# A mixture-of-experts layer with one Strassen level: a fourth of the first layer's block products taken by seven products of its own blocks, and squares of four slot tiles turned in one instruction

## The chip, the cores and the metric

The kernel runs on one core of one Trainium2 chip, in float32. The metric is the device time in microseconds (us) of one execution. Before the change it is 1579.84 us, the median of 3 runs (1579.2 to 1580.43).

## The reference

What is computed, cut to what matters: every token's vector of 512 is rotated as a set of quaternions (a 4 x 4 linear map of its four quarters of 128), a gate picks 2 of 8 experts for it, each expert takes up to 1024 tokens through two layers, and the weighted results are added to the input.

```python
# x: (4, 1024, 512); N = 4096 tokens, E = 8 experts, K = 2, D = 512, H = 2048
x_filtered = ifft(fft(x_quat, axis=1) * spectral_gate, axis=1).real    # gate is constant in time
x_rotated  = hamilton(q_left_n, hamilton(x_filtered, q_right_conj))    # 4 x 4 map per quarter
logits = xf @ gate_w.T
topv, topi = top_k(softmax(logits), K);  gates = topv / sum(topv)
cap = int(K * ((N + E - 1) // E))                                      # 1024 slots per expert
loc, valid = place of each choice in its expert's slots, loc < cap
de = slots filled with the rotated tokens                              # (E, cap, D)
h  = relu(einsum('ecd,ehd->ech', de, fc1_w) + fc1_b)                   # (E, cap, H)
eo = einsum('ech,ehd->ecd', h, fc2_w) + fc2_b                          # (E, cap, D)
out = x + sum over k of gates * valid * eo[slot of choice k]
```

## The kernel before

**Groups and products.** Each expert's hidden dimension of 2048 is cut into 4 groups of 512 (g = 0 to 3), so there are 32 groups, numbered k = 0 to 31, k = 4 e + g. In each group both layers are one level of Strassen's scheme: a matrix is cut into 2 x 2 blocks, and seven block products, numbered 0 to 6, take the place of eight. Group 0 alone takes its first layer in plain products (`layer1_plain`, L967). A scheme needs four sums of blocks on each side: `left1` (L133 to L143, GpSimd) makes them of the first layer's weights, the tiles `s`; `Slots.factors` makes those of the expert's rotated tokens with `sums` (L120, GpSimd) once per expert; `right2` (L190, also by `sums`, L126 to L129, tiles `t`) makes those of the second layer's weights. The sums on the hidden side, s1 to s4, are made by `chain` (L816 to L822, VectorE, lines L818 to L821) out of the first layer's blocks h11, h21, h22 and r12 (1024 columns each in two halves m = 0, 1).

**The first layer of a group**, `layer1` (L887), is a generator of 14 units. Units 0 and 1 take product 0 (`half`, L894 to L903, its matmuls at L896: 128 x 128 weights against 512 columns) and ScalarE writes it with its bias to h11 (L911). Products 5 and 6 go on into the same two PSUM banks a[0] and a[1] in units 2, 3 and 4, 5, each written out by ScalarE, to r12 and h21. Units 6 and 7 take product 4 into banks b, which VectorE adds to r12 (L918) and to h22 (L919). Products 1, 3 and 2 are not whole block products: each is again taken by seven products of the blocks of its own blocks, with 256 columns each. The class `Within` (L829) does this in four steps on one PSUM bank: `one` (2 products), `two` and `third`, `three`, `four` (2 products), all matmuls at L839, and after each its adds by VectorE at L850, seven in all. The bank's half a is used by `one`, then `two`, `three` and `four` accumulate on, so a step waits for the adds of the step ahead of it. A further bank c holds `third` of two such products side by side, in halves of one tile. The sums that these inner products need are made by `left_sub` (L147, GpSimd, tiles `sub13` and `sub2`, lines L162 to L165) and, once per expert, by `right_sub` (L172, VectorE, tiles `xsub`, L182 to L185). Products 1 and 3 run as a pair in units 8 to 11, product 2 follows in units 10 to 13.

**The second layer**, `second_layers` (L1125), is a second generator. It takes a group in two halves, st0 = 0 and 2, of seven units each: product 1 (with the add at L1165), 5 (L1169), 4, 6 (L1191, L1193), then product 0 of the next half (`start`, L1131, add at L1137), 3 (L1217) and 2 (L1220). All its matmuls are at L805, 256 columns each, and one unit is four of them. Product 0 of group k starts at unit 0 of the first layer of group k + 1: the second layer is one group behind.

**The order.** No scheduler orders the instructions; the program order is the order of the engines' queues. The main loop (L1246 to L1254) takes one unit of the first layer, then one of the second, and so on. After each of these half units it calls `turn(n)`, which pops n items of the list `background` and always one of the list `fetches`. `background` holds VectorE work: the four sums of `chain`, put at its head; the weighing and the store of finished rows (`Rows.store`: L681 on VectorE, then a scatter, L686, an indirect DMA issued by GpSimd); and the steps that rotate the next expert's tokens (`Slots.steps`): for half = 0, 1 of the slots and each quarter j of four, `squares(j)` turns four tiles of 128 x 128, one for each slot tile, into the one bank of the pool ps_x (L736), and then for i = 0 to 3 the bank, weighted by a number of the map, is written (j = 0: ScalarE, L774) or added (VectorE, L776) to part i of the rotated tokens. `fetches` holds indirect gathers issued by GpSimd: the next expert's rows in quarters (L721), the choices (L662) and the rows of the output (L632), to which the weighed results are added before they go back. How many items of `background` go where is a table, `PACE` (L1235 to L1239), of three rows (the first for k % 4 = 0 and for k = 1, the second for other k with k % 4 = 1, the third for k % 4 = 2 and 3), by unit, and by which of the two generators has just run. (In groups 0 and 31 one is popped each time.)

**What stands where around the change.** With g the group of the first layer: the steps of half 0 are appended to `background` at unit 11 of g = 1, those of half 1 at unit 9 of g = 2 (L1102). The finished rows of an expert, whose last group the second layer ends in the next expert's g = 0 and g = 1, are popped as stores by the same list. The quarters are appended to `fetches` at unit 12 of g = 0 and of g = 1 (L1100), the choices where the second layer begins its group 1 (L1151). `left_sub` of group k is called ahead of that group's units, one step after each of units 0 to 7 (L1086), with the steps of `right_sub` two by two in units 2 to 7 where g = 0 or k = 1 (L1088); the steps of `left1` for the group after are called in units 10 to 13, in g = 3 each with one of `Slots.factors` (L1105). Of `right2` for the next group, the first three sums are called just ahead of product 0 of that group (L1199) and the fourth after product 2 (L1222).

**Buffers.** SBUF: the rows gathered for a slot tile lie in 8 rotating tiles of 128 x 512 (`xgp`, L615, L630), `hidden` in 11 tiles of two banks' width (`unused`, L644: a block's tile is handed back by its last reader), w1 and w2 in two each, all sums on the left in one each. PSUM: the pool ps_1 has 4 banks (a, b, and those of `Within`), ps_2 3 banks (second layer), ps_x one bank.

Of the kernel before, what the change touches and what calls it, by code (L numbers as in the profile page):

```python
# [38 lines left out]
P = 128  # L40
D = 512
# [25 lines left out]
def kernel(  # L67
# [79 lines left out]
    def left_sub(k, w, s4):  # L147

        G = nc.gpsimd
        both = wsum.tile([P, 2, 4, P], F32, tag="sub13", name=f"sub13_{k}")  # L150
        one = wsum.tile([P, 1, 4, P], F32, tag="sub2", name=f"sub2_{k}")
        factors, steps = {}, []
        for t, block, names in ((both, w[:, :, 1], (1, 3)), (one, s4.unsqueeze(1), (2,))):

            def b(m, c, block=block):
                return block[:, :, c, m * P : (m + 1) * P]

            def q(i, t=t):
                return t[:, :, i]

            steps += [
                lambda b=b, q=q: G.tensor_tensor(q(0), b(1, 0), b(1, 1), ALU.add),  # L162
                lambda b=b, q=q: G.tensor_tensor(q(1), q(0), b(0, 0), ALU.subtract),
                lambda b=b, q=q: G.tensor_tensor(q(2), b(0, 0), b(1, 0), ALU.subtract),
                lambda b=b, q=q: G.tensor_tensor(q(3), b(0, 1), q(1), ALU.subtract),  # L165
            ]
            for n, name in enumerate(names):
                order = (b(0, 0), b(0, 1), q(3), b(1, 1), q(0), q(1), q(2))
                factors[name] = [f[:, n] for f in order]
        return factors, steps  # L170

    def right_sub(pool, e, right):  # L172

        factors, steps = {}, []
        for n in (1, 3, 2):
            t = pool.tile([P, 4, HS], F32, tag=f"xsub{n}", name=f"xsub{n}_{e}")

            def b(c, h, block=right[n]):
                return block[:, c, h * HS : (h + 1) * HS]

            steps += [
                lambda b=b, t=t: V.tensor_tensor(t[:, 0], b(0, 1), b(0, 0), ALU.subtract),  # L182
                lambda b=b, t=t: V.tensor_tensor(t[:, 1], b(1, 1), t[:, 0], ALU.subtract),
                lambda b=b, t=t: V.tensor_tensor(t[:, 2], b(1, 1), b(0, 1), ALU.subtract),
                lambda b=b, t=t: V.tensor_tensor(t[:, 3], b(1, 0), t[:, 1], ALU.subtract),  # L185
            ]
            factors[n] = [b(0, 0), b(1, 0), b(1, 1), t[:, 3], t[:, 0], t[:, 1], t[:, 2]]
        return factors, steps
# [426 lines left out]
    xgp = ctx.enter_context(tc.tile_pool(name="xgp", bufs=8))  # L615
# [13 lines left out]
    def gather(e, st, src):  # L629
        t = xgp.tile([P, D], F32, tag="rows", name=f"rows_{e}_{st}")  # L630
        s = e * SLOTS + st
        nc.gpsimd.indirect_dma_start(  # L632
            out=t,
            out_offset=None,
            in_=src,
            in_offset=bass.IndirectOffsetOnAxis(ap=slot_tok[:, s : s + 1], axis=0),
        )
        return t
# [12 lines left out]
    class Rows:  # L651
# [17 lines left out]
        def gather_rows(self, st):  # L669
            assert self.e == E - 1 or STORED.index(st) in turned_of[self.e + 1]  # L670
            self.rows[st] = gather(self.e, st, out)
# [27 lines left out]
    class Slots:  # L699


        def __init__(self, e):
# [5 lines left out]
            self.xg = {}  # L708
            self.rotated = 0

        def gather(self, half):
            self.xg[half] = [gather(self.e, st, x) for st in range(half * PER, (half + 1) * PER)]

        def gather_quarters(self, half, st, q):

            if q == 0:
                assert self.e == 1 or STORED[half * PER + st] in stored[self.e - 2]
                t = xgp.tile([P, D], F32, tag="rows", name=f"xq_{self.e}_{half}_{st}")
                self.xg.setdefault(half, []).append(t)
            s = self.e * SLOTS + half * PER + st  # L720
            nc.gpsimd.indirect_dma_start(  # L721
                out=self.xg[half][st][:, q * P : (q + 1) * P],
# [12 lines left out]
        def turn_squares(self, half, j, st, t):  # L735
            V.transpose(  # L736
                t[:, st * P : (st + 1) * P].rearrange("p (q w) -> p q w", w=CW),
# [564 lines left out]
```

## Time and profile before

One profiled execution of the program, taken by the hardware profiler:

| | |
|---|---|
| median of 3 runs (range) | 1579.84 us (1579.2 to 1580.43) |
| the profiled execution's own time | 1579.49 us |
| its span, first to last instruction | 1577.7 us |
| mean granted clock of TensorE in it | 0.987 |
| matmul pieces at L805 (second layer, 256 columns) | 3584 (1536, 1016, 512, 504 and 16 at the end) |
| of these the group a<-t,hidden | 364.1 us busy, 380 ns each |
| matmul pieces at L896 (512 columns), a<-x,s | x496, 592 ns each |
| weight loads, all groups shown | 190 or 191 ns each |
| L138 to L141, the sums of `left1` (GpSimd, 128 x 512) | 31 of each, 1.27 to 1.28 us |
| L126 to L129, the sums of `right2` (GpSimd, 128 x 512) | 32 of each, 1.52 to 2.06 us |
| L162, `left_sub` on two blocks (GpSimd, 128 x 256) | x31, 1.24 us |
| L721, quarters (GpSimd, indirect DMA) | x224, 1.03 us of issue each, 2.5 us from issue to landing |
| L818 to L821, `chain` (VectorE, 128 x 1024) | 32 of each, 1.55 to 1.86 us |
| L1165, L1193, L1220 and others of the second layer (VectorE) | 0.69 us each |

How to read it: the busy time of an engine counts its data instructions, the share is of the span. Matmuls overlap in TensorE's pipeline, so that one's duration (380 ns for 256 columns) is longer than the distance to the next. Every matmul of the program in float32 shows as two pieces in the trace, each with a weight load (PEld) of its own. "x" ahead of a number counts pieces or instructions. "<-PE w L839" behind an idle time names what the engine waited for: the tile w written by TensorE at line 839; "<-issue" is time in which it waited for nothing that the profile shows. Tile names are cut to the program's name without its number: w is the bank of a `Within`, c that of a pair, a and b the banks of whole products, `hidden` any block of the hidden layer, `sub` and `xsub` the inner sums, s and t the outer ones.

From 82.3 us, where the preparation (gate, choice and places of the tokens) is over, to about 1540 us TensorE runs through the 31 groups with no break that the trace shows beyond about 0.25 us at one place in each expert; an expert takes 188.2 us, a group 47.05 us.

### The profile page before, as it was taken

To read this page: it belongs to the slowest core of one execution; us is meant where nothing else is said; L and a number is where in the kernel's file an instruction comes from. 1 tells how busy PE (TensorE), PEld (TensorE's weight loads), DVE (VectorE), ACT (ScalarE), POOL (GpSimd) and SP (SyncE) were. 2 spreads that over 40 slices of the span, in tenths; PEclk is the share of its full clock that TensorE was granted. 3 is DMA by queue.
4 is the path that set the end of the run, shared out by engine and by line. 5 is a ranking of instruction groups with operands and counts; after the bars stand their busy time and mean duration, and the time that the engine had idled before them with its cause. 6 is when DMAs were issued, how large, how long until landed. Compare 5 with 4: busy or idle time off the path is not lost.

```text
span 1577.7 us, 17039 instructions
## 1 busy us (share of the span) xinstructions
PE 1544.9 (98%) x6221; PEld 1155.3 (73%) x6221; DVE 1175.9 (75%) x2082; ACT 283.7 (18%) x390; POOL 1076.5 (68%) x993
## 2 busy tenths in 40 slices
PE   5899999999999999999999999999999999999997
PEld 3667777777777777777777777777777777777776
DVE  6569877698776887688776887768867688776655
ACT  3222211112112111122111221111211121111110
POOL 1677676886768856788468866688576886665415
PEclk7899999999999999999999999999999999999999
DMA  8442112321221213220133210332122221321003
GB/s 322 160 173 77 54 45 91 117 76 54 100 94 63 73 54 114 103 99 14 53 122 121 83 56 10 124 113 81 54 82 78 92 72 54 114 106 39 16 27 105
DMA packets 48012, 137.46 MB, mean 87 GB/s; under 512 B 9335, under 2 KB 9591, under 8 KB 42809
## 3 DMA queue, kind: packets, MB, share of 16 engines
q1 hardware_dynamic: 22800, 75.54, 13.0%
q0 software_dynamic: 20736, 52.32, 10.5%
q10 hardware_dynamic: 4392, 8.52, 1.4%
q8 instruction: 49, 0.80, 0.2%
q14 instruction: 35, 0.28, 0.1%
HBM read 119.77 MB, written 25.23 MB: 92 GB/s over the span
## 4 chain that ended last, share of the span: by engine, by line
PE 95%; DMA 2%; issue 1%; POOL 1%; DVE 1%; SPq 0%; POOLq 0%; DVEq 0%
PE a L805 27%; PE b L805 20%; PE a L896 20%; PE w L839 13%; PE b L896 7%; PE c L839 5%; PE p L986 2%; DMA xb<-in_xt_dram 1%; DMA rows<-out_dram,slot_tok 0%; POOL rows L632 0%; POOL out_dram L686 0%; DMA rows<-in_x_dram,slot_tok 0%; SPq L229 0%; DVE A L504 0%; PE tok_ps L515 0%
## 5 line engine op out<-in xcount | busy, mean ns | idle before, releaser
L805 PE MATMUL a<-t,hidden 128*128 128x256 f32 x1536 | 364.1, 380 | 0.8 <-DVE v L1191 0.8
L805 PEld LDWEIGHTS a<-t,hidden 128*128 128x128 f32 x1536 | 292.7, 191 | 80.6 <-issue 40.7
L721 POOL DMA_INDIRECT xq<-in_xq_dram,quarter x224 | 231.0, 1031 | 56.1 <-issue 45.8
L805 PE MATMUL b<-w,hidden 128*128 128x256 f32 x1016 | 240.5, 380 | 2.4 <-DVE acc L1217 2.4
L805 PEld LDWEIGHTS b<-w,hidden 128*128 128x128 f32 x1016 | 193.2, 190 | 55.1 <-issue 27.7
L896 PE MATMUL a<-x,s 128*128 128x512 f32 x496 | 233.1, 592 | 0.0
L911 ACT ACTIVATE hidden<-a,b_sb 128x512 f32<-128x512 f32 x186 | 127.9, 688 | 575.2 <-PE a L896 575.2
L850 DVE TENSOR_TENSOR hidden<-w,hidden 128x256 f32<-128x256 f32 x465 | 191.0, 419 | 46.6 <-PE w L839 42.4
L827 ACT ACTIVATE hidden<-hidden 128x1024 f32<-128x1024 f32 x93 | 98.4, 1058 | 605.7 <-DVE hidden L850 357.6
L896 PEld LDWEIGHTS a<-x,s 128*128 128x128 f32 x496 | 94.2, 190 | 66.1 <-issue 59.8
L686 POOL DMA_INDIRECT out_dram<-rows,slot_add x64 | 66.6, 1041 | 109.9 <-DVE rows L681 99.1
L805 PEld LDWEIGHTS a<-w,hidden 128*128 128x128 f32 x512 | 97.3, 190 | 39.7 <-issue 29.7
L805 PE MATMUL a<-w,hidden 128*128 128x256 f32 x512 | 121.0, 379 | 0.0
L805 PE MATMUL b<-t,hidden 128*128 128x256 f32 x504 | 119.1, 379 | 0.0
L141 POOL TENSOR_TENSOR s<-w,s 128x512 f32<-128x512 f32 x31 | 39.5, 1276 | 115.3 <-PE w L839 115.1
L896 PE MATMUL b<-x,s 128*128 128x512 f32 x248 | 116.5, 592 | 0.0
L896 PE MATMUL a<-xa,w 128*128 128x512 f32 x248 | 116.4, 592 | 0.0
L805 PEld LDWEIGHTS b<-t,hidden 128*128 128x128 f32 x504 | 95.8, 190 | 26.2 <-issue 14.6
L138 POOL TENSOR_TENSOR s<-w 128x512 f32<-128x512 f32 x31 | 39.6, 1278 | 98.3 <-PE b L896 98.1
L839 PE MATMUL w<-xsub,sub 128*128 128x256 f32 x372 | 105.6, 379 | 0.0
L918 DVE TENSOR_TENSOR hidden<-b,hidden 128x512 f32<-128x512 f32 x62 | 42.5, 685 | 72.7 <-PE b L896 72.7
L850 DVE TENSOR_TENSOR hidden<-c,hidden 128x256 f32<-128x256 f32 x186 | 78.6, 423 | 21.3 <-PE c L839 15.8
(213 smaller groups left out, 2412.6 us busy)
## 6 DMA issues: line engine op xcount, KB each, us to landing
w<-in_w_dram SPq DMA_DIRECT2D x64, 1024.0 KB, 7.4
xb<-in_xt_dram SPq DMA_DIRECT2D x8, 1024.0 KB, 12.2
out_dram<-in_x_dram ACTq DMA_DIRECT2D x1, 8192.0 KB
xq<-in_xq_dram,quarter POOLq DMA_INDIRECT x224, 2.5
b<-in_b_dram POOLq DMA_DIRECT2D x8, 256.0 KB, 3.6
c<-choice,slot_cho POOLq DMA_INDIRECT x64, 2.3
rows<-out_dram,slot_tok POOLq DMA_INDIRECT x64, 3.6
out_dram<-rows,slot_add POOLq DMA_INDIRECT x64, 2.8
```

The lines of the kernel that those rows point to most:

```text
L138: lambda: G.tensor_tensor(s[0], w[:, 1, 0], w[:, 1, 1], ALU.add),
L141: lambda: G.tensor_tensor(s[3], w[:, 0, 1], s[1], ALU.subtract),
L686: nc.gpsimd.indirect_dma_start(out=out_of[st], out_offset=bass.IndirectOffsetOnAxis(ap=slot_add[:, s : s + 1], axis=0), in_=self.rows[st], ...
L721: nc.gpsimd.indirect_dma_start(out=self.xg[half][st][:, q * P : (q + 1) * P], out_offset=None, in_=xq, in_offset=bass.IndirectOffsetOnAxis ...
L805: nc.tensor.matmul(out[m] if isinstance(out, list) else out[:, m], lhsT=factors[0][n][:, c, (st0 + m) * P : (st0 + m + 1) * P], rhs=factor ...
L827: nc.scalar.activation(h, h, AF.Relu)
L839: nc.tensor.matmul(out, lhsT=self.left[n], rhs=self.right[n], start=first, stop=True, skip_group_check=True,)
L850: V.tensor_tensor(to, out, to, ALU.add)
L896: nc.tensor.matmul(out, lhsT=factors[0][n][:, c, m * P : (m + 1) * P], rhs=factors[1][n][:, c, :], start=first and c == 0, stop=c == 1, sk ...
L911: nc.scalar.activation(to[:, m], a[m], AF.Identity, bias=bias[:, m : m + 1])
L918: V.tensor_tensor(r12[:, m], b, r12[:, m], ALU.add)
L986: nc.tensor.matmul(ps[n][m][:, at], lhsT=w[:, block, i // 2, i % 2, m * P : (m + 1) * P], rhs=x.of(half, i)[:, at], start=i == 0 and at.st ...
```

## The change

**Products.** Product 6 of the first layer, so far a whole block product, becomes the fourth that is taken by seven products of its own blocks. It now forms a pair with product 1, in units 4 to 7 (`pair((1, h11), (6, h21))`); product 4 moves from units 6 and 7 to units 8 and 9; a second pair of products 3 and 2 takes units 10 to 13. After product 5 the bank a[m] is read twice by ScalarE, into r12 with one bias and into h21 with the other.

```diff
-        taken = []
-        for n, bias in ((0, lo), (5, lo), (6, hi)):
-            to = unused.pop(0)
-            taken.append(to)
-            for m in range(2):
-                half(a[m], m, n, n == 0)
-                nc.scalar.activation(to[:, m], a[m], AF.Identity, bias=bias[:, m : m + 1])
-                yield
-        h11, r12, h21 = taken
+        h11 = unused.pop(0)
+        for m in range(2):
+            half(a[m], m, 0, True)
+            nc.scalar.activation(h11[:, m], a[m], AF.Identity, bias=lo[:, m : m + 1])
+            yield
+        r12, h21 = unused.pop(0), unused.pop(0)
+        for m in range(2):
+            half(a[m], m, 5, False)
+            nc.scalar.activation(r12[:, m], a[m], AF.Identity, bias=lo[:, m : m + 1])
+            nc.scalar.activation(h21[:, m], a[m], AF.Identity, bias=hi[:, m : m + 1])
+            yield
+
+        def pair(*of):
+
+            p, q = (Within(h, subs[0][n], subs[1][n], f"w{n}_{k}") for n, h in of)
+            p.one()
+            q.one()
+            p.one_added()
+            q.one_added()
+            yield
+            c = bank1(f"c{of[0][0]}_{k}")
+            p.two()
+            p.third(c[:, :HS], True)
+            q.two()
+            q.third(c[:, HS:], False)
+            p.two_added()
+            q.two_added()
+            yield
+            p.three()
+            q.three()
+            p.three_added()
+            q.three_added()
+            yield
+            p.four()
+            q.four()
+            p.four_added()
+            q.four_added()
+
+        yield from pair((1, h11), (6, h21))
+        relu(h11)
+        yield
         h22 = unused.pop(0)
...
+        yield from pair((3, h21), (2, r12))
         relu(h21)
```

**Inner sums.** `left_sub` now makes the four sums of one block at a time (128 x 128, GpSimd), for the products 1, 6, 3 and 2 (tiles `sub1`, `sub6`, `sub3`, `sub2`); `right_sub` likewise on VectorE, with product 6 added. Those for 1 and 6 are called a group ahead, in units 9 to 13 of the group before; those for 3 and 2 in units 2 to 9. The sums of `left1` come in units 8, 9, 10 and 13, in the order 3rd, 1st, 2nd, 4th.

```diff
+        lefts, right_subs = {}, {}
+        TURN_OF_SUM = {8: 2, 9: 0, 10: 1, 13: 3}
...
+                for n, block, turns in ((3, w1_of[k][:, 1, 1], (2, 3, 4, 5)), (2, left_f[2], (6, 7, 8, 9))):
+                    lefts[n], more = left_sub(k, n, block)
+                    later(more, turns)
                 if k == 1 or g == 0:
-                    right_subs, more = right_sub(xtp, e, xf)
...
+                    for n, turns in ((6, (2, 2, 3, 3)), (3, (4, 4, 5, 5)), (2, (6, 7, 8, 9))):
+                        right_subs[n], more = right_sub(xtp, e, n, xf[n])
+                        later(more, turns)
...
+                    if i == 8 and k + 1 < NK:
+                        lefts[1], more = left_sub(k + 1, 1, w1_of[k + 1][:, 0, 1])
+                        later(more, (9, 10, 11, 12))
+                        lefts[6], more = left_sub(k + 1, 6, left_n[6])
+                        later(more, (10, 11, 12, 13))
+                        if g == NG - 1:
+                            right_subs[1], more = right_sub(xtp, e + 1, 1, xf_n[1])
+                            later(more, (8, 9, 9, 12))
...
-                if i in (10, 11, 12, 13):
-                    assert per == 1 or nxt.rotated == 2 * NJ
-                    for f in steps[:per]:
-                        f()
-                    steps = steps[per:]
+                if k and left_n and i in TURN_OF_SUM:
+                    steps[TURN_OF_SUM[i]]()
+                if k and fill_n and i >= 10:
+                    assert nxt.rotated == 2 * NJ
+                    fill_n.pop(0)()
```

Here `later(steps, turns)` puts each step behind the unit given for it.

**Squares.** The 8 rotating tiles of rows become two tiles of four slot tiles each, and the four turns of a quarter become one instruction of 128 x 512:

```diff
-    xgp = ctx.enter_context(tc.tile_pool(name="xgp", bufs=8))
+    xgp = ctx.enter_context(tc.tile_pool(name="xgp", bufs=1))
...
+    slots_of = [xgp.tile([P, PER, D], F32, name=f"rows{half}") for half in range(2)]
...
-        def turn_squares(self, half, j, st, t):
+        def turn_squares(self, half, j, t):
             V.transpose(
-                t[:, st * P : (st + 1) * P].rearrange("p (q w) -> p q w", w=CW),
-                self.xg[half][st].rearrange("p (q j w) -> p j q w", q=QT, j=NJ)[:, j],
+                t.rearrange("p (a w) -> p a w", w=CW),
+                slots_of[half].rearrange("p s (q j w) -> p j (s q) w", q=QT, j=NJ)[:, j],
             )
...
-                for st in range(PER):
-                    self.turn_squares(half, j, st, bank[j])
+                self.turn_squares(half, j, bank[j])
```

**Order.** In `chain`, r12's tile is handed back after s3 instead of s4. The choices' gathers are appended at g = 2 instead of g = 1, `right2`'s first three sums are called after product 3 (L1217) instead of ahead of product 0 of the next group, and the table is new:

```diff
-            if g == 1 and st0 == 0:
+            if g == 2 and st0 == 0:
                 r = rows[e] = Rows(e)
...
-    LATE = [(0, 0), (0, 1), (0, 0), (0, 1), (0, 1), (0, 1)]
     PACE = (
-        [(1, 1)] * 2 + [(1, 0)] * 4 + [(0, 0)] * 3 + [(0, 1), (0, 0), (0, 0), (0, 1), (0, 1)],
-        [(1, 1)] * 6 + [(0, 1), (1, 0)] + LATE,
-        [(1, 1)] * 2 + [(2, 2)] * 4 + [(0, 1), (1, 0)] + LATE,
+        [(1, 1), (1, 0)] + [(0, 1)] * 2 + [(0, 0), (0, 1)] + [(0, 0)] * 5 + [(0, 1), (0, 1), (0, 1)],
+        [(1, 1)] * 4 + [(0, 1), (1, 1), (0, 0)] + [(0, 1)] * 4 + [(1, 1)] + [(0, 1)] * 2,
+        [(1, 1), (1, 1), (2, 2), (2, 2), (0, 1), (2, 2), (0, 0), (0, 1), (1, 1), (1, 1), (0, 1)]
+        + [(1, 1), (0, 1), (0, 1)],
     )
```

In the program this makes the following of the counts: matmuls 3166 to 3259, VectorE's tensor_tensor 1421 to 1670, its transposes 226 to 58, GpSimd's tensor_tensor 535 to 783; ScalarE's instructions and the DMAs stay the same in number.

## The prediction

> **What bounds the kernel now.** I read the page from the top: busy shares, the clock row, the chain that ended last.
>
> ```profile
> span 1577.7 us, 17039 instructions
> PE 1544.9 (98%) x6221; PEld 1155.3 (73%) x6221; DVE 1175.9 (75%) x2082; ACT 283.7 (18%) x390; POOL 1076.5 (68%) x993
> PEclk7899999999999999999999999999999999999999
> PE 95%; DMA 2%; issue 1%; POOL 1%; DVE 1%; SPq 0%; POOLq 0%; DVEq 0%
> ```
>
> PE is on the chain for 95% of the span and its clock is full except at both ends. Since matmul ends are modelled, I next take starts, from the timeline of PE in a middle group:
>
> ```profile
> 699.10 1.89 PE L805 MATMUL b<-w,hidden 128*128 128x256 f32 x8
> 700.83 1.88 PE L896 MATMUL a<-x,s 128*128 128x512 f32 x4
> 702.55 1.89 PE L805 MATMUL b<-w,hidden 128*128 128x256 f32 x8
> 704.27 1.88 PE L896 MATMUL a<-x,s 128*128 128x512 f32 x4
> ```
>
> Start to start, eight 256-wide pieces take 1.72-1.73 us (215 ns each) and four 512-wide ones 1.72 us (430 ns each); one matmul of the program is two pieces. There is no gap, so PE streams and price goes by columns. What the other engines have left is read by stretches, one per group of an expert (g = 3, 0, 1, 2):
>
> ```profile
> 549.10:596.10 47.00, 47.00 (x188) 35.34 (x187) 38.47 (x67) 8.46 (x11) 25.36 (x20) 1.00 0.12 45
> 596.10:643.20 47.10, 47.10 (x188) 35.47 (x187) 35.31 (x60) 7.30 (x9) 32.55 (x30) 1.00 0.32 108
> 643.20:690.20 47.00, 47.00 (x187) 34.98 (x186) 31.39 (x53) 7.99 (x10) 40.25 (x40) 1.00 0.29 103
> 690.20:737.30 47.10, 47.10 (x188) 35.29 (x187) 40.31 (x71) 10.19 (x14) 39.84 (x39) 1.00 0.21 65
> ```
>
> The columns after the length are PE, PEld, DVE, ACT and POOL. DVE (40.3 of 47.1 in g = 2) and POOL (40.3 of 47.0 in g = 1, before some 0.16 to 0.30 us of issue per indirect DMA) are near full just where the new work goes. How close DVE is to making PE wait is seen in g = 2, where PE's four-step (L880, L881) needs the adds of L850:
>
> ```profile
> 725.76 1.40 DVE L736 STREAM_TRANSPOSE xps<-xq 128x128 f32<-128x128 f32 x4
> 728.29 0.42 DVE L850 TENSOR_TENSOR hidden<-c,hidden 128x256 f32<-128x256 f32 x1
> 728.41 0.59 PE L839 MATMUL w<-xsub,w 128*128 128x256 f32 x2
> 728.86 0.67 PE L839 MATMUL c<-xa,sub 128*128 128x256 f32 x2
> 729.37 0.59 PE L839 MATMUL w<-xsub,w 128*128 128x256 f32 x2
> ```
>
> The squares delay the adds; the add from c ends at 728.71, the c matmul has its slot at 728.84, and 728.86 to 729.37 is 0.51 us instead of 0.43. So PE wants an add about 0.25 us before the slot. Another such place loses 0.25 us per expert.
>
> **The change, part by part.**
>
> *PE.* Product 6 leaves L896: 4 matmuls of 512 columns, 8 pieces x 430 ns = 3.44 us. Seven of 256 come, 14 x 215 = 3.01 us. That is 0.43 us in each of 31 groups: **-13.4 us**, certain as long as PE streams. A rule speaks against this: the Trainium skill, "TensorE: Matmul & The Clock Gate", Part 3, The mechanism, says that weight loads overlap matmuls in flight only when their row group differs, and all of these are full 128-row loads. By it the 6 more loads per group would show, 6 x 190 ns (PEld rows) x 31 = +35 us, which would turn the gain into a loss of 22. The rows above speak otherwise: loads of 190 ns hide inside 215 ns pieces.
>
> *ACT.* As many instructions; but r12 and h21 are now both read from a[m] in units 2 and 3, one 0.69 us read more there.
>
> *DVE.* 7 more adds per group, by
>
> ```profile
> L850 DVE TENSOR_TENSOR hidden<-w,hidden 128x256 f32<-128x256 f32 x465 | 191.0, 419 | 46.6 <-PE w L839 42.4
> L736 DVE STREAM_TRANSPOSE xps<-xq 128x128 f32<-128x128 f32 x224 | 72.9, 325 | 7.5
> L776 DVE SCALAR_TENSOR_TENSOR xa<-xps,M,xa 128x512 f32<-128x512 f32 x84 | 59.1, 744 | 0.7
> ```
>
> cost 217 x 0.42 = 91 us of DVE; 32 more sums of the right side (0.41 each when alone, L184) 13 us. The squares: 4 x 128 columns take 1.40 us. No 512-wide turn is in the trace; it lies between one 128-wide (0.33) and four (1.40). The 256-wide turn at L394 took 0.45 against 0.33, so about 0.12 us per 128 columns: I take 0.71. That saves 56 x 0.69 = 39 us. Net +65 us, where DVE is free for some 400 (1577.7 - 1175.9): on average it holds. The question is the order in its queue. Pair (1, 6) now sits in units 4 to 7, where the slot work is popped by (2, 2) turns; before, pairs came in units 8 to 13, with 0 or 1.
>
> I run through g = 2 by hand, t = 0 at unit 2, each half unit 1.72 us, DVE instructions following each other 0.08 us before the last one's end (0.69 counts 0.61, 0.744 counts 0.66, a pair of adds 0.79). The square for j = 1 must wait until ACT has read the only ps_x bank; that last read is queued behind the two reads of a[0], which wait for product 5's first half: 1.72 + 0.2 + 3 x 0.6 = 3.8. Then square 0.73, L1220 0.61, four adds of L776 2.64, L1165 0.61, square 0.73, L776 0.66, the first two adds of the pair 0.79: 10.57. PE's two-step has its slot at 6 x 1.72 = 10.33 and wants 0.25 more: **late by 0.5**. DVE has no break until the adds of the three-step: 0.79 + 0.61 + 0.66 + 0.7 + 1.32 + 1.39 later come four adds of 1.58, end at 17.6; the c matmul, whose one tile holds both halves, has its slot at 10.83 + 1.72 + 1.72 + 0.86 + 1.72 + 0.43 = 17.28: **late by 0.6**. In g = 3 the same queue stands without the ACT wait at its head (0.5), in g = 0 the weigh at L681 (0.89) lies before the second pair's adds (0.3). These two are estimates by likeness. 1.9 per expert x 7 = 13.3, less the 0.25 x 7 = 1.7 lost now: **+11.6**. Bounds: -1.7 (every add in time) and +31 (a 512-wide turn at 1.40: two more times 0.69 at both places in g = 2, one at g = 3).
>
> *POOL.* Per group four 256-wide sums (1.24, 1.10, 1.09, 0.78) become eight 128-wide ones (0.48) and four more come: +1.6 us. Behind them waits the chain that ends in sub2's second sum, which p2's two-step needs in g = 1:
>
> ```profile
> 632.72 1.00 POOL L686 DMA_INDIRECT out_dram<-rows,slot_add  x1 [10.11 <-DVE rows L681]
> 640.79 1.01 POOL L686 DMA_INDIRECT out_dram<-rows,slot_add  x1 [2.03 <-DVE rows L681]
> 664.02 0.97 POOL L721 DMA_INDIRECT xq<-in_xq_dram,quarter  x1 [1.30 <-DMA out_dram<-rows,slot_add]
> 678.77 0.47 POOL L163 TENSOR_TENSOR sub<-sub,s 128x128 f32<-128x128 f32 x1
> ```
>
> From the first scatter to the end of that sum POOL takes 679.24 - 632.72 = 46.5 us, almost without a break; PE asks at 683.18 (730.23 less one group of 47.05), 50.4 us after the scatter. After the change the first store is popped in unit 11, not 9 (-6.9), the two-step asks 0.9 sooner and the group is 0.4 shorter: 42.2 us are left. The work: 46.5, less three of left1's sums now done ahead of it (-3.8), less sub13's four (-3.3), plus seven 128-wide sums (+3.3), plus two more quarter gathers in the stretch (16 for 14, 1.26 each, +2.5) = 45.2, or 41.9 without the two waits in it (2.03 and 1.30). Late by -0.3 to 3.0; I take the middle, 1.4, for the 6 experts with stores and quarters in g = 1: **+8.4**, bounds 0 and +26 (3.0, and 1.3 more where right2's second sum, moved back a unit, has 2.3 us of cover left).
>
> *Costed at nothing.* right2's first three sums one unit later: t1 ended at 653.0 for a product at 658.7, cover 5.7, left 2.3; without it the 1.3 just named. The gather of the choice one group later: weights need it some 40 us on. SP's loads are issued at the same points; they land in 7.4 us, first read in unit 8. The eight sums more before k = 1 (3.8 us) lie in POOL's 7.7 us wait ahead of the x sums. The tail keeps its order.
>
> **Sum.** -13.4 + 11.6 + 8.4 = +6.6 on the profiled execution's 1579.5 us (span 1577.7 and 1.8 around it; the median of the runs is 1579.84): **1586 us**.
>
> **Rivals.** (1) *DVE and POOL keep up, PE streams on*: 1579.5 - 13.4 = **1566**. For it: DVE idles 15% even in g = 2, and POOL's sums moved out from beside DVE's chain (L818 to L821 took up to 2.7 us beside POOL's, 1.2 alone), which could bring DVE 1 us forward. Against: the hand run. It decides if both places in g = 2 have 0.6 us more and POOL 1.4. (2) *POOL in time, DVE late*: 1579.5 - 13.4 + 11.6 = **1578**, no change to be told. For it: the two waits in POOL's stretch need not recur. (3) *POOL far behind*: +26 in place of 8.4, and DVE as summed: **1604**. For it: 40.3 of 47 busy before anything is added; against: three sums left the stretch. (4) *The wide turn costs nearly as much as four narrow ones*: DVE at +31, so **1605**. Against: the 256-wide row.
>
> **Numbers.** The forecast 0.42, rival 1 0.20, rival 2 0.18, rival 3 0.14, rival 4 0.06. A measurement of this kernel can tell about 0.2%, 3.2 us. Faster: rival 1 and a third of rival 2, 0.25; same: 0.15; slower 0.60. The likeliest case alone would be 1582 to 1595; the range 1566 to 1602 reaches to rival 1 and nearly to rival 3.
>
> **What would show it.** L839 with 1736 or so pieces and L896's form a<-x,s at half its count; groups of 46.6 us where nothing is late. Idle PE weight loads "<-DVE hidden" in units 5 and 7 of g = 2 would show the DVE step, "<-POOL sub" in g = 1 the POOL step. Groups of 46.6 us throughout would make me wrong, and so would a 512-wide turn of under 0.5 us or PE pieces above 215 ns.

## The result and the profile after

The changed kernel took 1583.99 us (median of 9 runs, 1581.53 to 1586.85), the kernel before beside it 1579.20 us (9 runs, 1577.71 to 1580.43): ratio 1.003, interval 1.002 to 1.004. It is slower by 0.3%, 4.8 us, where 1586 was forecast. The profiled execution has a span of 1581.3 us, 3.6 more than before. The rows of its page that answer to those shown of before, and the row of the wide turn from its groups by form:

```profile
span 1581.3 us, 17588 instructions
PE 1538.8 (97%) x6407; PEld 1190.2 (75%) x6407; DVE 1224.1 (77%) x2163; ACT 276.9 (18%) x390; POOL 1123.8 (71%) x1241
PE 80%; DVE 9%; POOL 5%; issue 2%; DMA 2%; ACT 1%; SPq 0%; POOLq 0%; DVEq 0%
L724 DVE STREAM_TRANSPOSE xps<-rows 128x512 f32<-128x512 f32 x56 | 40.4, 722 | 13.8 <-ACT xa L762 13.1
```

The chain of waits says it at once: TensorE held 95% of it, now 80%; VectorE has 9% and GpSimd 5%. VectorE's busy time grew by 48.2 us; the lengths of its instructions, which overlap a little, add up to 64.2 us more (net +65 was forecast). The wide turn takes 0.72 us (0.71 was taken).

Where the time went is read from the lengths of the groups. Each is the distance between the starts of two products 0 (the first a<-xa,w pieces of a group in TensorE's timeline), as a mean over six experts, k = 4 to 27; in brackets the extremes where they differ by over 0.1:

```
length of a group, us      g = 1                  g = 2                  g = 3    g = 0
before                     47.22                  47.07                  46.97    46.97
after                      48.29 (48.14 to 48.83) 47.58                  46.72    46.83
stores_early               47.28 (46.89 to 47.67) 47.58                  46.72    46.56
pace_g2                    48.21 (48.14 to 48.33) 46.56                  46.56    46.83
sub2_early                 48.30 (48.01 to 48.78) 47.58                  46.72    46.83
clean                      47.32 (46.84 to 47.91) 46.56                  46.56    46.56
clean_sub2                 46.70 (46.56 to 47.29) 46.56                  46.56    46.56
clean_both                 47.71 (47.41 to 47.98) 46.56                  46.66    46.56
clean_narrow               47.35 (46.99 to 47.87) 48.01 (47.94 to 48.15) 46.56    46.56
narrow                     49.69 (48.74 to 50.59) 49.63                  48.08    46.83
control (= after)          48.60 (48.15 to 50.55) 47.58                  46.72    46.83
pace_look (= pace_g2)      48.78 (48.16 to 50.51) 46.56                  46.56    46.83
before_look (= before)     47.22                  47.65 (47.29 to 47.95) 46.97    46.97
wide_alone                 46.97                  47.47 (47.12 to 47.76) 46.97    46.97
```

A group with no wait is 46.56 us long against 46.97: 0.41 us less, as the smaller products should bring. But g = 1 gained 1.1 us and g = 2 0.5. The first place, in g = 1, in the timelines of TensorE and of GpSimd after the change (start, duration, engine, line, operation):

```profile
682.12 0.59 PE L830 MATMUL w<-xsub,sub 128*128 128x256 f32 x2
682.55 0.60 PE L830 MATMUL c<-xsub,sub 128*128 128x256 f32 x2
684.51 0.70 PE L830 MATMUL w<-xsub,sub 128*128 128x256 f32 x2 [1.37 <-POOL sub L156]
```

```profile
680.61 0.47 POOL L158 TENSOR_TENSOR sub<-w,sub 128x128 f32<-128x128 f32 x1
681.24 0.96 POOL L709 DMA_INDIRECT rows<-in_xq_dram,quarter  x1 [0.16 <-issue]
682.51 0.94 POOL L709 DMA_INDIRECT rows<-in_xq_dram,quarter  x1 [0.30 <-issue]
683.46 0.46 POOL L155 TENSOR_TENSOR sub<-s 128x128 f32<-128x128 f32 x1
684.00 0.45 POOL L156 TENSOR_TENSOR sub<-sub,s 128x128 f32<-128x128 f32 x1
```

The two pieces of w at 684.51 stand at 682.55 + 0.43 = 682.98 when nothing holds them: 1.53 us late. What they want is the second sum of sub2 (sub<-sub,s), which ends at 684.45, behind two gathers. In the six experts the same distance is 1.48 to 2.04 us, 9.6 us in all. (The piece after such a wait comes another 0.1 us late.)

The second place, in g = 2, in the timelines of TensorE and VectorE:

```profile
716.86 0.60 PE L830 MATMUL w<-xsub,w 128*128 128x256 f32 x2
717.87 0.70 PE L830 MATMUL c<-xa,sub 128*128 128x256 f32 x2 [0.41 <-DVE hidden L841]
```

```profile
714.72 0.73 DVE L724 STREAM_TRANSPOSE xps<-rows 128x512 f32<-128x512 f32 x1
715.48 0.75 DVE L764 SCALAR_TENSOR_TENSOR xa<-xps,M,xa 128x512 f32<-128x512 f32 x1
717.38 0.42 DVE L841 TENSOR_TENSOR hidden<-c,hidden 128x256 f32<-128x256 f32 x1
```

The c matmul starts 1.01 us after the w pieces instead of 0.43, because the last of the four adds (717.38) has a turned square and a weighted add (714.72, 715.48) ahead of it: 0.57 us, in each of six experts. Ahead of the two-step of the same pair 0.24 us are lost.

### The profile page after: what moved, and what is told of

It reads as the page before. It is cut to its first block, busy times and chain, and to the rows that moved or that the text cites. A ratio compares the mean times of both kernels' runs of the same rounds, so it can differ in the third digit from the quotient of the medians.

```text
span 1581.3 us, 17588 instructions
## 1 busy us (share of the span) xinstructions
PE 1538.8 (97%) x6407; PEld 1190.2 (75%) x6407; DVE 1224.1 (77%) x2163; ACT 276.9 (18%) x390; POOL 1123.8 (71%) x1241
## 4 chain that ended last, share of the span: by engine, by line
PE 80%; DVE 9%; POOL 5%; issue 2%; DMA 2%; ACT 1%; SPq 0%; POOLq 0%; DVEq 0%
PE a L793 24%; PE b L793 16%; PE w L830 14%; PE a L887 12%; PE c L830 6%; PE b L887 6%; DVE xa L764 3%; POOL rows L709 2%; DVE hidden L841 2%; PE p L974 2%; POOL out_dram L676 1%; DMA xb<-in_xt_dram 1%; DVE xps L724 1%; POOL rows L622 0%; DMA rows<-out_dram,slot_tok 0%
## 5 line engine op out<-in xcount | busy, mean ns | idle before, releaser
L841 DVE TENSOR_TENSOR hidden<-w,hidden 128x256 f32<-128x256 f32 x620 | 253.9, 418 | 67.1 <-PE w L830 61.2
L709 POOL DMA_INDIRECT rows<-in_xq_dram,quarter x224 | 234.0, 1044 | 58.3 <-issue 49.6
L830 PE MATMUL w<-xsub,sub 128*128 128x256 f32 x496 | 138.8, 382 | 9.1 <-POOL sub L156 8.6
L841 DVE TENSOR_TENSOR hidden<-c,hidden 128x256 f32<-128x256 f32 x248 | 104.7, 422 | 23.2 <-PE c L830 18.9
L887 PE MATMUL a<-x,s 128*128 128x512 f32 x248 | 116.6, 592 | 0.0
L830 PEld LDWEIGHTS w<-xsub,sub 128*128 128x128 f32 x496 | 93.4, 190 | 26.0 <-POOL sub L156 11.1
L764 DVE SCALAR_TENSOR_TENSOR xa<-xps,M,xa 128x512 f32<-128x512 f32 (+1 forms) x108 | 71.0, 684 | 4.2 <-ACT xa L762 3.0
```

The source lines that it names most:

```text
L709: nc.gpsimd.indirect_dma_start(out=slots_of[half][:, st, q * P : (q + 1) * P], out_offset=None, in_=xq, in_offset=bass.IndirectOffsetOnAxi ...
L764: V.scalar_tensor_tensor(to, t, M[:, i, j : j + 1], to, ALU.mult, ALU.add)
L830: nc.tensor.matmul(out, lhsT=self.left[n], rhs=self.right[n], start=first, stop=True, skip_group_check=True,)
L841: V.tensor_tensor(to, out, to, ALU.add)
L887: nc.tensor.matmul(out, lhsT=factors[0][n][:, c, m * P : (m + 1) * P], rhs=factors[1][n][:, c, :], start=first and c == 0, stop=c == 1, sk ...
```

## The experiments

The times are medians; the kernel before was run beside each. It did not take the same time on all chips (1579.2 to 1586.1 us), so ratios to it are compared with care, and the groups above decide.

**stores_early.** Stores of finished rows are popped earlier in g = 0.

```diff
-        [(1, 1), (1, 0)] + [(0, 1)] * 2 + [(0, 0), (0, 1)] + [(0, 0)] * 5 + [(0, 1), (0, 1), (0, 1)],
+        [(1, 1), (1, 0)] + [(0, 1)] * 2 + [(0, 0), (0, 1)] + [(0, 0)] * 2 + [(0, 1)] * 2 + [(0, 0)] * 2 + [(0, 1)] * 2,
```

> The changed kernel with one edit: in the first row of the pace table the stores of finished rows are popped in units 8, 9, 12 and 13 of the expert's first group instead of 11, 12 and 13. Theory (GpSimd is late in g = 1 because its run of scatters and gathers starts late, and the sums of sub2 stand behind it): the wait before the two-step of product 2, 1.5 us in each of 5 experts and 2.0 in a sixth, goes; 1584.0 - 9.6 = about 1574 us. Rival (GpSimd has too much work in that group, wherever it starts): the wait stays at half or more, 1579 us or above. Second rival (the earlier stores delay VectorE's adds in units 8 to 10 of g = 0): 1584 or above, with new waits on hidden there.

Measured: 1576.11 us (1574.51 to 1577.34), 0.9956 of before (0.9944 to 0.9968; before 1582.56). g = 1 fell from 48.29 to 47.28 and g = 0 from 46.83 to 46.56. First scatter of the changed kernel's run, and the same of this kernel with the wait that is left:

```profile
640.57 1.02 POOL L676 DMA_INDIRECT out_dram<-rows,slot_add  x1 [5.86 <-DVE rows L671]
```

```profile
630.72 1.02 POOL L676 DMA_INDIRECT out_dram<-rows,slot_add  x1 [2.17 <-DVE rows L671]
680.55 0.70 PE L830 MATMUL w<-xsub,sub 128*128 128x256 f32 x2 [0.75 <-POOL sub L156]
```

The run starts 6.8 us earlier in its expert (35.57 us after the start of g = 0, in place of 42.35; 10 us in the program's time), and the wait falls to 0.2 to 1.0 us, from 9.6 to 3.7 in the six experts. The 7.9 us less than the changed kernel's first median are between the 9.6 of the theory and the first rival's bound of 5; the groups give 6 x 1.28 = 7.7. Of these only 6.1 are GpSimd's, in g = 1. The other 1.6 are VectorE's, in g = 0, and the theory did not have them: in the changed kernel a weighing (L671) stands ahead of a pair's adds there and costs 0.27 us. The start of the run is the main cause of GpSimd's wait. What is left of it is not shown to be work, for the earlier run stands still in two places, where the changed kernel's run waits 0.65 us for a landing:

```profile
639.07 1.00 POOL L676 DMA_INDIRECT out_dram<-rows,slot_add  x1 [2.41 <-DVE rows L671]
662.11 0.97 POOL L709 DMA_INDIRECT rows<-in_xq_dram,quarter  x1 [3.28 <-DMA out_dram<-rows,slot_add]
```

**pace_g2.** Three rotation steps of VectorE moved out of units 3 and 5.

```diff
-        [(1, 1), (1, 1), (2, 2), (2, 2), (0, 1), (2, 2), (0, 0), (0, 1), (1, 1), (1, 1), (0, 1)]
+        [(1, 1), (1, 1), (2, 2), (1, 2), (0, 1), (1, 1), (0, 1), (0, 1), (2, 2), (1, 1), (0, 1)]
```

> The changed kernel with one edit: in the third row of the pace table (g = 2 and 3) three of VectorE's rotation steps are taken out of units 3 and 5, one of them goes to unit 6 and two to unit 8. Theory (VectorE's adds for the pair in units 4 to 7 are late because rotation steps stand before them): the waits of 0.57 us on the shared c tile and of 0.24 us before the two-step, in six experts, go: 1584.0 - 6 x 0.81 = about 1579 us; the GpSimd wait in g = 1 stays at 1.5. Rival (VectorE is full there and the wait only moves, to product 4's banks or to the second pair): no change, 1583 to 1585.

Measured: 1586.83 us (12 runs, 1575.91 to 1588.30), 1.0017 of before (1.0002 to 1.0032). By the median a miss, by the profile not: in its profiled execution (1575.91 us) g = 2 is 46.56 and g = 3 46.56, every wait for VectorE in these two is gone, g = 0 keeps its 0.27 us, and g = 1 stays at 48.2. Most of its other executions were 10 us longer with a mean clock of 0.983 to 0.985 in place of 0.989; (0.989 - 0.983) x 1580 = 9.5 us.

**clean.** Both edits.

> The changed kernel with both edits of the pace table at once. Theory (two separate causes that add up, and TensorE streams at 215 ns a piece otherwise): 1584.0 - 9.6 - 4.9 = 1569.5, and down to 1566 (1579.5 - 13.4) if the small waits of 0.1 to 0.2 us go with them; groups of 46.6 us. Rival (weight loads or something else at the small matmuls eat the gain of 0.43 us per group, and the waits are only where it shows): not under 1575, with matmul pieces of the pairs above 215 ns start to start.

Measured: 1568.91 us (1568.52 to 1569.68), 0.9911 of before (0.9898 to 0.9924). As the theory had it: the two causes add up, and three groups of four are 46.56 us.

**narrow.** The wide turn undone.

```diff
-            V.transpose(
-                t.rearrange("p (a w) -> p a w", w=CW),
-                slots_of[half].rearrange("p s (q j w) -> p j (s q) w", q=QT, j=NJ)[:, j],
-            )
+            for st in range(PER):
+                V.transpose(
+                    t[:, st * P : (st + 1) * P].rearrange("p (q w) -> p q w", w=CW),
+                    slots_of[half][:, st].rearrange("p (q j w) -> p j q w", q=QT, j=NJ)[:, j],
+                )
```

> The changed kernel with one part undone: the squares of four slot tiles are turned in four instructions of 128 x 128 again instead of one of 128 x 512 (0.72 us in the trace of the changed kernel against 1.40 for four). Theory (VectorE's queue in units 2 to 7 of g = 2 and 3 sets the lateness of the pair): each square adds 0.68 us; the two-step's 0.24 becomes about 1.6, the wait on c 0.57 about 1.2 in g = 2, and g = 3 gets waits of its own of up to 1 us: 1584.0 + 12 to 21, that is 1596 to 1605. Rival (VectorE is only 77% busy and takes it up): 1584 to 1587.

Measured: 1617.22 us (1612.99 to 1618.25), 1.0213 of before (1.0197 to 1.0229): 33 us more, not 12 to 21. Two of its waits, and the stretches around the first (length, then busy time of PE, PEld, DVE, ACT and POOL, granted clock, DMA share, GB/s):

```profile
697.93 0.70 PE L831 MATMUL w<-xsub,sub 128*128 128x256 f32 x2 [1.95 <-POOL sub L156]
727.19 0.70 PE L831 MATMUL w<-xsub,sub 128*128 128x256 f32 x2 [1.44 <-DVE hidden L842]
```

```profile
694.50:698.50 4.00, 2.05 (x10) 1.47 (x10) 1.02 (x2) 0.00 (x0) 3.45 (x6) 1.00 0.17 49
698.50:702.00 3.50, 3.50 (x11) 2.83 (x10) 1.64 (x5) 1.27 (x2) 3.50 (x6) 0.57 0.01 2
```

The two-step of g = 2 is 1.6 us late (start to start), exactly as worked out. Two things were not: g = 3 lost 1.36 us against the changed kernel by its group length (48.08 for 46.72), and GpSimd's wait in g = 1 grew to 2.1 us; its first scatter stands as far ahead of the waiting pieces' place as before (42.5 us, 42.4 in the changed kernel), but the sixteen gathers of quarters behind it take 17.2 to 17.7 us of GpSimd's time, in place of 16.7, because one to three of them take 1.5, 1.25 and 1.1 us and not 0.95. The one wait of 2.04 us in the changed kernel comes after the same three (17.7). Why they take longer is open. The first expert's groups, outside the table, lost 4.9 us more. And after such a wait the clock stood at half for 3.4 us (0.57 in the second stretch, 11 pieces in it where 16 would go): some 1.7 us more, in three of the six experts.

**control and pace_look.** The changed kernel and pace_g2 once more, on another chip.

> The changed kernel without any edit, beside the same runs of the kernel before as the next ones, since the kernel before took 1582.6 us where the four earlier kernels were run and 1579.2 us at first. Expected if the ratio is what holds: 1.003 times the kernel before, within 0.002; if the kernel before has merely drifted, the changed one stays at 1584 and the ratio falls to 1.001.

> The same kernel as pace_g2, to see an execution of the longer kind: 8 of its 12 took 1585 to 1588 us with a mean clock of 0.983 to 0.985, the others 1576 to 1582 with 0.987 to 0.989. Theory (the wait for GpSimd in g = 1, now 1.5 to 1.7 us, can let the clock fall to half for 3.4 us, as after the 2.1 us waits of the kernel narrow): up to six stretches at half clock just after those waits, 1.7 us each, 10 us in all. Rival (the clock rises later in the preparation): the low stretch before 60 us is 20 us longer, none in between.

Measured: control 1584.49 us (1582.09 to 1588.41), which is the changed kernel's 1584; but the kernel before took 1586.06 there, so that the ratio is 0.9992 (0.9981 to 1.0003). pace_look took 1580.85 us. Both profiled executions have one half-clock stretch in their middle, behind a wait for GpSimd of about 2 us (first control, then pace_look; for each a row of the timeline, and then the stretch after it):

```profile
686.12 0.70 PE L830 MATMUL w<-xsub,sub 128*128 128x256 f32 x2 [1.90 <-POOL sub L155]
```

```profile
686.80:690.20 3.40, 3.40 (x12) 2.70 (x11) 1.10 (x2) 1.26 (x2) 3.40 (x6) 0.59 0.00 0
```

```profile
305.90 0.93 PE L830 MATMUL w<-xsub,sub 128*128 128x256 f32 x2 [1.86 <-POOL sub L156]
```

```profile
306.00:309.40 3.40, 3.40 (x9) 2.72 (x10) 1.10 (x2) 1.26 (x2) 3.40 (x5) 0.53 0.00 0
```

pace_look has a second wait as long, at 1249.50 (1.87 us of idle time), after which the clock stayed full; its other four, of 1.2 to 1.4 us of idle time, were not followed by one either. That is the theory of pace_look with one stretch in place of six; an execution at 0.983 was not caught, so that its stretches lie there too is likely and not shown.

**sub2_early.** The place of sub2 in GpSimd's queue alone.

```diff
-... (2, left_f[2], (6, 7, 8, 9))):
+... (2, left_f[2], (3, 4, 5, 6))):
```

> The changed kernel with one edit: the four GpSimd sums of sub2 come in units 3 to 6 instead of 6 to 9, so ahead of some scatters and gathers, with as much work in all. Theory (GpSimd is late in g = 1 by the start of its run, all its sums for the second pair stand at the end of it): the wait turns to another sum of the same pair, sub3's, and half or more of it stays: 0.997 to 1.000 of the changed kernel. Rival (only the place of sub2 in the queue is wrong): the wait of 9.6 us goes as in stores_early, 0.994 of the changed kernel or less.

Measured: 1581.75 us (1579.33 to 1582.34), 0.9965 of before (0.9953 to 0.9977), 0.9983 of the changed kernel. The wait for sub is gone and g = 1 is as long as it was, 48.30. The theory named the wrong heir, though. GpSimd, VectorE and TensorE in that kernel:

```profile
683.32 0.94 POOL L709 DMA_INDIRECT rows<-in_xq_dram,quarter  x1 [0.31 <-issue]
...
686.25 0.73 DVE L724 STREAM_TRANSPOSE xps<-rows 128x512 f32<-128x512 f32 x1 [3.22 <-DMA rows<-in_xq_dram,quarter]
686.89 0.67 DVE L1177 TENSOR_TENSOR v<-a,b 128x512 f32<-128x512 f32 x1
687.48 0.41 DVE L841 TENSOR_TENSOR hidden<-w,hidden 128x256 f32<-128x256 f32 x1
...
687.93 0.70 PE L830 MATMUL w<-xsub,w 128*128 128x256 f32 x2 [0.62 <-DVE hidden L841]
689.18 0.70 PE L830 MATMUL c<-x,sub 128*128 128x256 f32 x2 [0.55 <-DVE hidden L841]
```

The last quarter is gathered at 683.32, the first square of the next expert waits for it at the head of VectorE's queue for 3.22 us, and the pair's adds stand behind the square. What is late is GpSimd's run of scatters and gathers as a whole; sub2 was only the first to show it. (The 2.7 us by which it beats control are more than the groups show; control had a stretch at half clock.)

**wide_alone.** The second part of the change alone, on the kernel before.

> The kernel before with the second part of the change alone: two tiles of four slot tiles, and the four turns of a quarter in one instruction. Theory (VectorE loses TensorE only 0.25 us per expert before the change): 38 us less of VectorE, but the time falls by 1.7 us at most, ratio 0.9985 to 1.000. Rival (with two tiles for eight rotating ones, gathers wait for tiles still read): slower, ratio over 1.001, with new waits at the gathers. Second rival (VectorE's freed time shortens more than TensorE's waits show): below 0.998.

Measured: 1579.73 us (1578.36 to 1582.12), 0.9958 of before (0.9945 to 0.9972), beside a kernel before of 1586.06. The ratio is the second rival's. In the groups the 0.25 us of g = 1 are gone, 1.5 us for six experts, as the theory had it; that the rest of the ratio lies in the kernel before, which was longer on that chip than anywhere else, is likely and not shown: it was not profiled there.

**before_look.** The kernel before, profiled on a further chip.

> The kernel before itself, for a profile of it where it is slow: it took 1579.2 us beside the changed kernel at first, then 1582.6 and 1586.1 on two chips, at the same mean clock of 0.986 to 0.991, while the changed kernel kept 1584. Theory (the kernel before has a wait that is near its limit and differs from chip to chip, in VectorE's queue with the narrow squares, since wide_alone beside it took 1579.7): groups longer than 47.1 us in g = 1 or 2, with waits of TensorE in units 8 to 13, 0.5 to 1 us per expert. Rival (the preparation or the end is longer): the first group starts after 86 us or the last instruction comes later than 8 us after the last matmul, groups as before.

Measured: 1583.22 us; g = 2 is 47.29 to 47.95 long, 3.5 us more over the six experts, of a span 3.7 us longer than at first. VectorE and TensorE there:

```profile
918.78 0.87 DVE L850 TENSOR_TENSOR hidden<-w,hidden 128x256 f32<-128x256 f32 x2
921.51 0.69 DVE L1165 TENSOR_TENSOR acc<-b,v 128x512 f32<-128x512 f32 x1 [1.86 <-PE w L839]
...
923.34 0.67 PE L839 MATMUL w<-xsub,sub 128*128 128x256 f32 x2 [0.64 <-DVE hidden L850]
```

VectorE stood still for 1.86 us ahead of the add at L1165, with the adds for the pair behind it. TensorE had written its input (the last piece of b ended at 918.72), and the same add began at once in the first profile. It recurs in each expert, 1.2 to 1.9 us, and in wide_alone. The place is shown, the cause is not; wide_alone, which has the wide turn, has it too. The 0.3% of the result hold beside a kernel before that is free of it; where the kernel before took 1586 us there was no difference.

**clean_both.** Two moves of the change undone in clean: the choices at g = 1 again, right2's first three sums ahead of product 0 again.

```diff
-            if g == 2 and st0 == 0:
+            if g == 1 and st0 == 0:
...
                 rights[k + 1], more = right2(k + 1, loaded[k + 1])
+                for f in more[:3]:
+                    f()
...
-            if last_of_group and k + 1 < NK:
-
-                for f in more[:3]:
-                    f()
```

> The kernel clean with two moves of the change undone that the prediction cost at nothing: the choices' gathers are appended at group 1 of the second layer again, and the first three sums of right2 are called ahead of product 0 of the next group again. Theory (they are hidden): as clean, 0.991 of the kernel before as then measured, within 2 us. Rival (GpSimd in g = 1 and 2 has no room for eight gathers of 1.26 us more beside its sums, which is why they were moved): new waits for sub or t tiles, 4 us or more over clean.

Measured: 1572.13 us (1570.71 to 1573.65), 0.9933 of before (0.9919 to 0.9946; before 1582.63, as beside clean): 3.2 us over clean. Between the two: g = 1 is 0.39 and g = 3 0.10 longer, 6 x 0.49 = 2.9. That is more than the 2 us of the theory and less than the 4 of its rival, but of the rival's kind: the wait for sub in g = 1 is 0.7 to 1.3 us in all six experts, where clean has 0.2 to 1.2. The moves cost nothing, as the prediction assumed, and bring GpSimd some room, which it did not count.

**clean_narrow.** Narrow turns in clean.

> The kernel clean with the squares turned in four instructions again: what the first part of the change is worth with a table that suits it, and what the wide turn adds. Theory (VectorE's queue in units 2 to 7 is what limits; in narrow the two-step of g = 2 came 1.6 us late): about 1 to 2.2 us per expert in g = 2 and 3, so clean + 6 to 14 us. Rival (the table of clean leaves VectorE so much room that the wide turn is worth nothing): as clean, within 2 us.

Measured: 1579.54 us (1577.66 to 1581.25), 0.9979 of before (0.9969 to 0.9989; before 1582.63): 10.6 us over clean, most of it in g = 2 (48.01 for 46.56, 6 x 1.45 = 8.7); another 1.2 are in the first expert. Of the 13.7 us by which clean is under the kernel before, the wide turn brings 10.6 with this table, and the smaller products, without it, 3.1.

**clean_sub2.** sub2 earlier in clean.

> The kernel clean with the sums of sub2 in units 3 to 6 besides, as in sub2_early. In clean's profile TensorE still waits for sub2 in g = 1 of five experts, 0.3 to 1.25 us, 4 us in all; nothing else but the end of the kernel is above 0.5 us. Theory (GpSimd's run now starts early enough, so what is left is indeed only sub2's place at its end): the 4 us go, 0.9885 of the kernel before if that takes what it took beside clean (1582.6), about 1565 us. Rival (as in sub2_early the wait turns to sub3 and to VectorE's adds behind it): as clean, 1568 to 1570.

Measured: 1566.98 us (1564.51 to 1568.39), 0.9919 of before (0.9906 to 0.9933; before 1579.47 there). It beats both kernels, by 12.5 us and, against the changed one's 1583.99, by 17.0. With GpSimd's run started in time the wait had next to no heir: g = 1 is 46.56 to 46.58 in four of six experts, and the longest wait left is 0.6 us for VectorE's adds in one. TensorE in a pair:

```profile
702.27 1.03 PE L793 MATMUL a<-t,hidden 128*128 128x256 f32 x4
703.13 0.59 PE L830 MATMUL w<-xsub,sub 128*128 128x256 f32 x2
703.57 0.59 PE L830 MATMUL c<-xsub,sub 128*128 128x256 f32 x2
704.00 0.59 PE L830 MATMUL w<-xsub,sub 128*128 128x256 f32 x2
```

Two pieces every 0.43 us and four in 0.86, small products and second layer alike: there is no gap left to see.

## Why the prediction was right

**TensorE's price: right.** Summed as 0.43 us per group and -13.4; groups without a wait are 0.41 shorter, 31 x 0.41 = 12.7. (clean_sub2 is 12.5 under the kernel before of the same chip, but that holds small waits lost and won as well.) The small matmuls and their weight loads cost what their columns say: two pieces take 0.43 us. The +35 us of the rule on weight loads did not come.

**GpSimd: right in place and kind, a little small.** 1.4 us in six experts were summed, 8.4; 9.6 were measured, at the two-step of product 2 and for the second sum of sub2, and 10.4 by the length of g = 1 (6 x 1.73), with the slower restart of TensorE behind each wait. The run from the first scatter to that sum takes 43.9 us (640.57 to 684.45), between the 41.9 and 45.2 worked out, and has 42.4 us of room for 42.2. The first store popped two units later was in the sum as 6.9 us less room; starting it early again (stores_early) took most of the wait away.

**VectorE: right at g = 2, too large elsewhere.** Over six experts 1.9 us each had been taken.

- g = 2: the two-step 0.5 forecast, 0.24 measured; the shared c tile 0.6 forecast, 0.57 measured. With the slower restart of TensorE after each the group lost 1.02 us (47.58 - 46.56), for 1.1 forecast.
- g = 3: 0.5 forecast "by likeness", 0.16 measured. This step failed: "the same queue" does not stand there. By VectorE's timeline the second square comes ahead of the pair's first adds in g = 2 (708.36, the adds at 709.78) and behind them in g = 3 (758.97, the adds at 756.79).
- g = 0: 0.3 forecast, 0.27 measured.

That is 1.45 us per expert for 1.9, some 10 us for seven in place of 13.3. The 1.7 us of before that should vanish were 0.35 x 6 = 2.1. The upper bound of +31 does not follow from its words: five more times 0.69 in seven experts are 24 us, which makes +36. In narrow, which has the dear turns, g = 2 and g = 3 grew by 3.4 us per expert, five times 0.68.

**The sum.** -12.7 + 10.4 + 10 - 2.1 = +5.6, for +6.6 forecast. That it came so near is in part luck: VectorE's term was 3 us too large, GpSimd's 2 too small. The medians differ by 4.8 and the spans by 3.6, less than the sum, and the profiles show where the spans lose it. From the start of group 1 to that of group 31 the changed kernel is 5.8 us longer (1413.7 for 1407.9), but what comes after is 2.4 us shorter. One wait near the end left the clock of the kernel before at half for 3.4 us, and a like one in the changed kernel did not (before, then after; for each the wait, then a stretch behind it, with the columns as under narrow):

```profile
1544.89 2.56 PE L805 MATMUL b<-w,hidden 128*128 128x256 f32 x8 [2.42 <-DVE acc L1217]
1546.20:1549.50 3.30, 3.30 (x10) 2.59 (x9) 1.12 (x4) 0.00 (x0) 2.39 (x4) 0.50 0.65 200
1550.13 1.97 PE L793 MATMUL b<-w,hidden 128*128 128x256 f32 x8 [2.10 <-DVE acc L1222]
1551.40:1554.70 3.30, 3.30 (x17) 2.91 (x16) 1.81 (x5) 0.00 (x0) 2.39 (x4) 1.00 0.70 207
```

**The rivals.** The clean case was priced at 1566; it is what clean_sub2 measures, 1567.0. The condition put to it, 0.6 us for VectorE and 1.4 for GpSimd, is what the two table rows and the place of sub2 provide. The dear wide turn is out: 0.72 us. Had it come, 1605 would have been too little, for narrow took 1617: the bound was too low, and GpSimd's longer waits and the half clock behind them were not in it.

**Missing in the prediction:** that a wait can cost more than its length through the clock, and that the median of the kernel before is up to 7 us longer on some chips.

## What to carry to other kernels

When a bound engine is made shorter, its helpers' deadlines come earlier by as much; run the order of each helper's queue against them before counting the gain, in the stretch where the helper is fullest. If a wait vanishes by moving the instruction it names and the stretch is no shorter, as in sub2_early, the queue as a whole is late: look for what starts it. An arithmetic saving of 0.8% was there all the time, and seven entries of a table decided whether it was seen.

## What the runs showed of the hardware

A wait of TensorE's of about 2 us can halve its clock for the next 3.4 us, which costs 1.7 us more. Of ten waits of 2.0 to 2.1 us, start to start, in the middle of the profiled executions (six of narrow, two of pace_look, one each of after and control) five did so; none of those of 1.7 us or less did. At the end of the kernel a wait of 2.3 to 2.6 us did so in 7 of the 14 profiles. The Trainium skill, "TensorE: Matmul & The Clock Gate", section "Why this matters for your kernels", advises against idle gaps of more than about 3 us. Here 2 us were enough in half the cases. Such chance may be part of why one kernel's runs spread by up to 12 us.

An idle time of an in-order engine ahead of an instruction whose inputs are written, as VectorE's 1.2 to 1.9 us ahead of L1165 in before_look, was there in one profile of a kernel and not in another of the same kernel. It stays unexplained.
